# Layer 2's mixing: four stores and then four loads, or one store and one load by turns, on the transfer queue of a four-layer convolution kernel

## The chip, the cores and the metric

The kernel runs on one core of a Trainium2 chip. The metric is the device time of one execution, in microseconds. Before the change it is 4314.44 us, the median of 3 runs (4307.86 to 4318.33).

The core has five engines with a queue of instructions each: TensorE (PE in the profile, with its weight loads as PEld), VectorE (DVE), ScalarE (ACT), GpSimd (POOL) and SyncE (SP). They run side by side and wait for each other with semaphores. SP does no arithmetic here; it issues transfers, which 16 DMA engines then carry out. A transfer that has to wait holds up everything that stands behind it on SP.

## The reference

A tensor x of 16 samples, 16 channels and 256 x 256 points, in float32, goes through four layers. Each normalises x in groups (8 groups over 16 channels), convolves it in its own way and adds the result to x:

```
x = x + _L0_conv_ref(_gn(x), L0_conv_weight)          # 3x3, circular, by FFT in the reference
x = x + _L1_conv_ref(_gn(x), L1_conv_filter_w)        # five diagonal taps
x = x + _L2_conv_ref(_gn(x), ty, tx, poles, residues) # spectral layer with poles
x = x + _L3_conv_ref(_gn(x), weight, scale, bias)     # 3x3 on rounded inputs
```

The change lies in layer 2:

```
alpha = jnp.fft.fft2(x, axes=(-2, -1))
A = 1.0 / (omega1[:, None, None, None] - weights_pole1[None])
Bm = 1.0 / (omega2[:, None, None, None] - weights_pole2[None])
S = jnp.einsum('ikpq,oikp,xikq->oxik', weights_residue, A, Bm)
output_residue1 = jnp.einsum('biox,oxik->bkox', alpha, S)
...
x1 = jnp.fft.ifft2(output_residue1, s=(Ny, Nx), axes=(-2, -1)).real
```

At each frequency (o, x) the 16 input channels of every sample are mixed by a 16 x 16 complex matrix S(o, x), which is itself made of poles and residues. This mixing, output_residue1, is the stage that the change touches. A second term (x2, from C, D and output_residue2) is made elsewhere.

## The kernel before

The function layers holds the whole kernel as stages one after another: layers 0 and 1 together, sample by sample; layer 2's forward transform; layer 2's mixing; layer 2's way back; and layer 3.

The forward transform leaves alpha in a DRAM tensor alphad, by row frequency. There are 256 of these, as real and imaginary parts of the even and odd halves of the spectrum. The mixing takes them in NF = 64 blocks of 4. It writes the mixed spectrum to a DRAM tensor mixd, which the way back reads (tile ot, line 1148), so the way back begins only when the mixing's stores are done.

**One block of the mixing** (the loop over n from line 963). The block's data lie in a tile z, of which there are two, zs[0] and zs[1], used by turns. z has 128 partitions. The four frequencies of a block lie in every fourth partition, each in its own quarter of the columns, and the rest is zero, so that one product mixes four frequencies at once. Line 970 is this product:

```
nc.tensor.matmul(to, lhsT=sk[:, x_], rhs=z[:, :, x_], start=True, stop=True)
```

It runs for each of 129 column frequencies x_: 128 in the loop over at (32 steps of four), and one alone. Every product of a block reads all partitions of z, so a block's first product needs all four of its loads. After each 8 steps (g = 0 to 3) ACT copies half of the sums from PSUM (other, line 996) and DVE adds and subtracts (line 998, which the profile shows under the helper's line 190) into the output tile ob, of which there are two as well. POOL corrects a few elements of ob (lines 1007 to 1010).

**The mixing matrices** are made in the same loop, two blocks ahead, by the generator system: products of line 891, copied from PSUM into sk by ACT and DVE by turns (lines 899 to 908), with POOL copying one part (line 905). Another generator, poles, makes factors of the matrices on POOL and DVE. The loop advances both with next(...) between its own steps.

**The transfers of a block**, all on SP:

- load (lines 915 to 918) brings one of the four frequencies: alphad into z, 32 partitions by 2064 numbers, 258 KB. reload (lines 927 to 931) is the load with a marker ahead of it: DVE sets one element of z to zero (line 930), so the load waits until DVE has come to this place and the older products that read this z are done. During block n, reload fetches the data of block n + 1, into the z that block n does not use.
- leave (lines 920 to 925) stores a quarter of ob: 64 partitions by 1024 numbers, 256 KB, into mixd.

In the program's text they stand like this. For block n (from n = 1), after step group g = 0: reload(n + 1, 0), leave(n - 1, 1), reload(n + 1, 1), leave(n - 1, 2). After g = 1: reload(n + 1, 2), leave(n - 1, 3), reload(n + 1, 3). After g = 3: leave(n, 0). Below, S0 to S3 are the four stores of block n - 1 and L0 to L3 the four loads for block n + 1.

**What sets the order.** A scheduler may reorder each engine's instructions within what the data allow. A context, tc.manual_schedule, lists engines for which the order of the program's text is kept. In the mixing (line 935) the list names PE, DVE, ACT and POOL. SP isn't in it, so the scheduler sets SP's order. It puts the four stores of a block together and then the four loads:

```
L924 mixd<-ob x4     S0 S1 S2 S3 of block n-1
L917 z<-alphad x4    L0 L1 L2 L3 for block n+1, each waits for its marker on DVE
L924 mixd<-ob x4     the next block
```

Of the kernel before, what the change touches and what calls it, by code (L numbers as in the profile page):

```python
# [164 lines left out]
def layers(ctx, tc, x, w0, w1, w3, sw, bias, ty, tx, p1a, p1b, p1c, p2a, p2b, p2c, resa, resb,  # L165
# [695 lines left out]
    with ExitStack() as es:  # L861
# [65 lines left out]
        def reload(n, f):  # L927
# [5 lines left out]


        es.enter_context(tc.manual_schedule(engines={
            mybir.EngineType.PE, mybir.EngineType.DVE, mybir.EngineType.Activation, mybir.EngineType.Pool}))

        zs = [new(zp, [FB, NX, BG], f"z{k}") for k in range(2)]
        V.memset(zs[0][:, 0 : FB // 2], 0.0)
# [485 lines left out]
```

## Time and profile before

| what | value |
|---|---|
| median of 3 runs | 4314.44 us |
| the profiled execution's own time | 4332.44 us |
| its span | 4330.7 us |
| busy over the span: PE, DVE, ACT, POOL | 86%, 70%, 59%, 47% |
| mixing: first and last start of a product of line 970 | 2272.5 and 3013.4 us |
| transfers in the mixing: loads of z, stores of ob | 258, 256 |
| median time from issue to landing: loads, stores | 4.0 us, 4.5 us |
| the marker of line 930 on DVE | 59 ns |
| issue of a load, of a store on SP (median) | 478 ns, 590 ns |

How to read it: the profile is one execution. Its page gives each engine's busy time, groups of equal instructions by line, and for each group the idle time before it with the instruction or transfer that ended it ("releaser"). "issue" as a releaser means that nothing in the profile explains the wait. A transfer appears twice: as an instruction on SP's queue (the issue) and, by its semaphore, as the landing that others wait for. The views used further on are the page, the busy times in a stretch of time ("windows"), the waits by who waited for whom, the instructions in order of time, and the list of transfers. The first block (n = 0) reloads and stores nothing of this kind and the last (n = 63) loads nothing, so that 62 blocks (n = 1 to 62) have the full set of four stores and four loads.

### The profile page before, as it was taken

How to read it: one execution, taken by the hardware profiler on the slowest of the kernel's cores; microseconds unless marked ns; L12 is line 12 of the kernel's file. 1: busy time of each engine (PE TensorE's matmuls, PEld its weight loads, DVE VectorE, ACT ScalarE, POOL GpSimd, SP SyncE). 2: the span in 40 equal slices, each digit the busy share in tenths (PEclk: the TensorE clock that was granted, in tenths of full speed). 3: DMA queues.
4: the chain of work that ended last, by engine and by line, in shares of the span. 5: the costliest groups of instructions: out<-in, count | busy, mean ns of one | idle time of the engine just before them, and what ended most of it. 6: DMA issues, size and time to landing. Idle time of an engine off the chain costs nothing. (4 is left out here: it accounts for less than half of the span.)

```text
span 4330.7 us, 126404 instructions
## 1 busy us (share of the span) xinstructions
PE 3739.1 (86%) x52880; PEld 2882.1 (67%) x52880; DVE 3040.5 (70%) x5585; ACT 2573.2 (59%) x3641; POOL 2057.0 (47%) x3279
## 2 busy tenths in 40 slices
PE   4999999999967989999996777776899999996776
PEld 1455555555545989899985555555788888883444
DVE  4676667666659878787765566664567777768888
ACT  2868686776824434344446666665545544447898
POOL 2233232423244645564546666664566666662222
PEclk9999999999988999999999999998999999997989
DMA  6767676776633544444535666666878888877998
GB/s 141 172 154 191 142 192 150 183 169 155 158 89 117 164 144 144 139 152 157 162 113 167 182 194 183 185 192 174 228 217 239 237 244 235 247 206 273 343 351 295
DMA packets 479579, 820.78 MB, mean 190 GB/s; under 512 B 39648, under 2 KB 371424, under 8 KB 463584
## 3 DMA queue, kind: packets, MB, share of 16 engines
q1 hardware_dynamic: 431904, 644.63, 52.6%
q0 software_dynamic: 47104, 168.06, 13.0%
q8 instruction: 416, 6.82, 0.7%
q14 instruction: 155, 1.27, 0.1%
HBM read 408.85 MB, written 336.07 MB: 172 GB/s over the span
## 5 line engine op out<-in xcount | busy, mean ns | idle before, releaser
L382 PE MATMUL ps<-va,wt 128*64 128x512 f32 (+1 forms) x1632 | 668.7, 571 | 11.6 <-POOL va L354 9.2
L382 PE MATMUL ps<-vb,wt 128*64 128x512 f32 (+1 forms) x1632 | 667.1, 570 | 4.5 <-DMA vb<-va 4.5
L781 ACT ACTIVATE y<-ps_y,bc 128x384 f32<-128x384 f32 x512 | 296.4, 581 | 406.8 <-PE ps_y L779 406.6
L403 ACT ACTIVATE v<-xt,nm 32x2048 f32<-32x2048 f32 x248 | 497.2, 2005 | 9.8 <-PE ps L417 3.5
L417 PE MATMUL ps<-v,w1s 128*64 128x259 f32 x4096 | 486.4, 397 | 11.0 <-DVE v L401 6.7
L970 PE MATMUL ps_m<-z,sk 128*32 128x64 f32 x16384 | 334.5, 227 | 176.1 <-issue 126.5
L190 POOL TENSOR_TENSOR w<-rq 128x512 f32<-128x512 f32 x256 | 335.7, 1333 | 261.5 <-ACT rq L1115 259.4
L970 PEld LDWEIGHTS ps_m<-z,sk 128*32 128x32 f32 x16384 | 302.9, 114 | 227.2 <-issue 151.9
L382 PEld LDWEIGHTS ps<-va,wt 128*64 128x64 f32 x1632 | 223.1, 137 | 311.3 <-issue 283.3
L417 PEld LDWEIGHTS ps<-v,w1s 128*64 128x64 f32 x4096 | 338.9, 142 | 136.0 <-issue 27.9
L1114 PE MATMUL ps_o<-exp,fs 128*128 128x128 f32 x2048 | 399.6, 277 | 9.7 <-ACT fs L1162 9.7
L1113 PE MATMUL ps_o<-c_last,zt 128*128 128x128 f32 x2048 | 398.1, 276 | 0.0
L190 DVE TENSOR_TENSOR ob<-ps_m,other 128x256 f32<-128x256 f32 x512 | 192.9, 418 | 276.0 <-ACT other L996 262.4
L1259 PE MATMUL ps_c<-q,wt 64*64 64x512 bf16 (+1 forms) x4608 | 292.8, 405 | 108.6 <-ACT o L1306 91.7
L1113 PEld LDWEIGHTS ps_o<-c_last,zt 128*128 128x128 f32 x2048 | 323.2, 193 | 60.8 <-issue 60.8
L891 PE MATMUL ps_s<-t,l 128*32 128x258 f32 x4096 | 320.5, 401 | 42.3 <-issue 24.8
L190 POOL TENSOR_TENSOR acc<-acc,prod 128x256 f32<-128x256 f32 x240 | 232.8, 970 | 226.4 <-DVE prod L190 220.3
L1259 PEld LDWEIGHTS <-wt 64*64 64x64 bf16 x4800 | 181.6, 114 | 220.2 <-issue 152.8
L1114 PEld LDWEIGHTS ps_o<-exp,fs 128*128 128x128 f32 x2048 | 313.7, 194 | 11.3 <-ACT fs L1162 11.3
L776 PE MATMUL ps_y<-c_y,qd 128*128 128x128 f32 x2048 | 316.0, 277 | 1.6 <-ACT hat L738 1.6
L779 PE MATMUL ps_y<-hat,qd 128*128 128x128 f32 x2048 | 314.5, 276 | 0.0
L190 DVE TENSOR_TENSOR xt<-xt,ps 128x512 f32<-128x512 f32 x256 | 175.4, 685 | 187.6 <-PE ps L382 185.6
(234 smaller groups left out, 8897.9 us busy)
## 6 DMA issues: line engine op xcount, KB each, us to landing
xt<-x2d SPq DMA_DIRECT2D x256, 512.0 KB, 4.3
z<-alphad SPq DMA_DIRECT2D x258, 258.0 KB, 4.0
xt<-in_x_dram SPq DMA_DIRECT2D x256, 256.0 KB, 7.4
x2d<-x2s POOLq DMA_DIRECT2D x256, 256.0 KB, 5.0
mixd<-ob SPq DMA_DIRECT2D x256, 256.0 KB, 4.5
ot<-mixd SPq DMA_DIRECT2D x256, 256.0 KB, 6.2
x3d<-xt SPq DMA_DIRECT2D x128, 512.0 KB, 5.4
xt<-x3d SPq DMA_DIRECT2D x64, 1024.0 KB, 9.4
```

What stands on the lines that cost most here:

```text
L190: eng.tensor_tensor(o, a, b, op)
L382: nc.tensor.matmul(ps[halves[h], lo:hi, :], lhsT=wt0[:, w, :], rhs=v[:, 2 * t + lo : 2 * t + hi, j : j + N], start=j == 0 and k == 0, stop ...
L403: nc.scalar.activation(to, o.xt[c][q_], AF.Identity, bias=o.g.nm[q_, 1:2])
L417: nc.tensor.matmul(ps[halves[h], k, 0:U], lhsT=o.w1[:, w : w + 64], rhs=v1[:, lo : lo + U], start=first_, stop=not first_)
L776: nc.tensor.matmul(to[:, :, a, :], lhsT=v[:, c, a, i % 2, :], start=a == 0, stop=a == 1, rhs=y1[:, a].rearrange("p (r f) -> p r f", r=2))
L779: nc.tensor.matmul(ps[:, 2 * P : 3 * P], lhsT=v[:, c, a, i % 2, :], start=False, stop=a == 1, rhs=hats[0][:, a, i].rearrange("p r k -> p ( ...
L781: nc.scalar.activation(y[:, c, :], ps[:, 0 : 3 * P], AF.Copy, scale=bc2[:, b, i // 2, 0:1])
L891: nc.tensor.matmul(ps[at : at + 32, d, 0 : 2 * NX], lhsT=ls[h][:, k + d - k0, n], rhs=t2[:, h, k + d].rearrange("p r x -> p (r x)"), start ...
L970: nc.tensor.matmul(to, lhsT=sk[:, x_], rhs=z[:, :, x_], start=True, stop=True)
L1113: nc.tensor.matmul(ps[:, a, c, :], lhsT=zts[d][:, a, c, :], rhs=last[:, c, :], start=True, stop=False)
L1114: nc.tensor.matmul(ps[:, a, c, :], lhsT=fs[:, d, a, :], rhs=ey[:, d, c, :], start=False, stop=True)
L1259: nc.tensor.matmul(o, lhsT=wt[half[h], w, :], rhs=src, start=i == 0, stop=i == len(work[0]) - 1)
```

## The change

SP is added to the engines whose order is the program's own, in the mixing stage only. SP's order becomes S0 L0 S1 L1 S2 L2 S3 L3 for the blocks that have all eight, 62 of them; before these and after them the queue stands as before. The other engines keep the order of their instructions, and the rest of the kernel is not touched. Since one line is added, the lines behind it are one higher in the changed kernel's profile (L970 becomes L971; L917, L924 and L930 lie ahead of the added line and keep their numbers).

```
@@ -933,7 +933,8 @@
         es.enter_context(tc.manual_schedule(engines={
-            mybir.EngineType.PE, mybir.EngineType.DVE, mybir.EngineType.Activation, mybir.EngineType.Pool}))
+            mybir.EngineType.PE, mybir.EngineType.DVE, mybir.EngineType.Activation, mybir.EngineType.Pool,
+            mybir.EngineType.SP}))
```

The queue of the changed kernel, for a block:

```
L924 mixd<-ob     S0 of block n-1
L917 z<-alphad    L0 for block n+1, waits for its marker on DVE
L924 mixd<-ob     S1
L917 z<-alphad    L1, waits for its marker
L924 mixd<-ob     S2
L917 z<-alphad    L2, waits for its marker
L924 mixd<-ob     S3
L917 z<-alphad    L3, waits for its marker
```

## The prediction

> **What bounds the kernel now.** I read the page's head first, then its groups (which line belongs to which stage), then the stretch of the mixing alone, then in that stretch PE's waits and the transfer queue's order of time, and last single transfers.
>
> ```profile
> span 4330.7 us, 126404 instructions
> PE 3739.1 (86%) x52880; PEld 2882.1 (67%) x52880; DVE 3040.5 (70%) x5585; ACT 2573.2 (59%) x3641; POOL 2057.0 (47%) x3279
> ```
>
> The whole kernel is PE's, but the change touches one stage, from the first product of L970 (2272.5 us) to the last (3013.4 us). The windows view of that stretch has the busy times, in the order PE, PEld, DVE, ACT, POOL, then granted clock, DMA share, GB/s:
>
> ```profile
> 2272.00:3014.00 742.00, 531.80 (x20470) 429.56 (x20464) 435.91 (x1261) 496.06 (x1188) 451.71 (x1061) 0.96 0.63 183
> ```
>
> No engine is full: PE 72%, ACT 67%, DMA 63%. 64 blocks in 742 us are 11.6 us each, so a cycle of waits sets the pace. PE's waits from 2290 us to the stretch's end (total, times, longest):
>
> ```profile
> PE ps_m L970 <- issue: 126.5, 89, 3.9
> PE ps_m L970 <- ACT sk L908: 31.2, 30, 1.7
> PE ps_s L891 <- issue: 24.8, 19, 2.1
> PE ps_m L970 <- DMA z<-alphad: 15.0, 16, 2.2
> ```
>
> The largest is "issue", 151.3 us in 108 waits; the wait for z seems small. The queue's order of time and single transfers say more. One block, first the queue, then its fourth load alone, then that load's time to landing, then the first load's, then PE:
>
> ```profile
> 2601.99 3.12 SPq L924 DMA_DIRECT2D mixd<-ob  x4
> 2605.21 6.32 SPq L917 DMA_DIRECT2D z<-alphad  x4
> 2614.75 2.75 SPq L924 DMA_DIRECT2D mixd<-ob  x4
> ...
> 2611.09 0.45 SPq L917 DMA_DIRECT2D z<-alphad  x1
> ...
> z<-alphad SPq DMA_DIRECT2D x1, 258.0 KB, 2.9
> ...
> z<-alphad SPq DMA_DIRECT2D x1, 258.0 KB, 4.8
> ...
> 2614.11 0.89 PE L970 MATMUL ps_m<-z,sk 128*32 128x64 f32 x49
> ```
>
> The fourth load is issued at 2611.09, lands 2.9 us later at 2613.97, and 0.14 us after that the next block's first product starts. The loop is: a block's products, DVE's second pair of sums and the fourth marker (L930, at 2611.00), fourth load, next block. PE's wait table hides it, because other matmuls stand between and the gap is then written to another releaser. Taking the landing of every fourth load from the trace's semaphore events, 26 of 62 blocks start 0.13 to 0.14 us after it (28 within 0.25 us); the other 34 have 0.36 to 2.8 us of slack. So in nearly half of the blocks the last load's landing is the pace. It is issued 7.2 us after the block's start, at DVE's pace, and lands 3.5 us later in the mean; alone it would take 2.9, the rest is queueing.
>
> **The change part by part.** No compute instruction is added, removed or moved; PE, DVE, ACT and POOL keep their order. What moves is 3 of 4 stores in each of 62 blocks, on SP's queue alone (POOL issues no transfer in this stage, and the last block's four stores, which the next stage reads, stay where they are): S0 S1 S2 S3 L0 L1 L2 L3 becomes S0 L0 S1 L1 S2 L2 S3 L3.
>
> *Gain for the loads.* L0 no longer stands behind three stores' issue. Before, its marker comes 2.3 us after the block's start and its issue some 0.15 to 0.4 us later. But L0 isn't what the next block waits for; L3 is. Worth nothing, and no other cover is needed for it.
>
> *Issue time on SP.* L1, L2 and L3 each get one store issue (median 590 ns) ahead of them. L2 and L3 wait for markers 2.9 and 1.9 us after the one before, so these issues fit in. L1 comes some 0.5 us later and has 3 us to spare. Worth nothing for L3.
>
> *Stores are held by the loads' markers.* S1, S2, S3 wait behind L0, L1, L2 for DVE's L930. S0 goes at -0.3 us from the block's start as before; S1 moves from 0.3 to about 3.1, S2 from 0.9 to about 4.3, S3 from 1.6 to about 5.9. Before, four stores used the stretch from 0 to 5 us, in which no load can run yet; now only one does, and three quarters of a megabyte is put among the loads, ahead of L3. That is the cost. It needs the service time of a transfer in a full queue. From the block above: the fourth store lands 4.9 us after its issue (2603.78), 6.7 us after the first one's issue; less 3.05 for a lone transfer that is three services of 1.2 us. My estimate from the landings of all 62 blocks (mean miss 0.37 us) is a queue served in order, 3.05 us for a lone transfer, 1.2 us a store, 0.85 us a load. Then, from a block's start: L0 issued at 2.6, lands at 5.65; S1 6.85, L1 7.7, S2 8.9, L2 9.75, S3 10.95, L3 11.8. Before, L3 lands at 7.3 + 3.5 = 10.8. It comes 1.0 us later.
>
> Bounds of that delay. From below: the transfer packets' own time fills 63% of the engines, 7.2 us a block, 0.9 us for each of eight transfers. Six services of 0.9 after L0 give 11.05, and with an L0 at 2.4 about 10.9: +0.1 to +0.5. Nothing below zero: L3's issue is bound by the same marker, and the same bytes stand ahead of it, later. From above: replayed block by block with the fitted services, against the same replay of the old order, the mean delay is 1.55 us.
>
> Price: a block is pushed by the delay less its slack. With 1.0 us: 28 blocks by nearly 1.0 (27.8 us) and 19 blocks with slacks of 0.36 to 1.11 by the rest (8.7 us), 36 us. With 0.5 us: 15 us. With 1.5 us: 61 us.
>
> *What is won back.* [...] 151.3 of 742 us is a fifth, so I take a fifth off: 36 becomes 28 us. The ends are nothing (36) and a loop in which every block runs at the queue's floor of 11.8 + 0.14 us, against 11.55 now: 62 x 0.4 = 25 us, or 13 us with an L3 at 11.6.
>
> *Stores' release of ob.* ob has two buffers; block n+1's first sums wait for the four stores of block n-1. Before, these have 6.8 us to spare in the median, 5.0 at least. S3's landing moves by about 4.7 us (6.4 to 11.0), so 0.3 to 2 us are left. Taken as nothing; in the upper end it isn't.
>
> [...]
>
> [...]
>
> **Sum.** +28 us on the profiled execution, whose own time is 4332.4 us (span 4330.7), 18 us above the median of the runs, 4314.4. On the median: 4342 us, 0.65% slower. About 0.3%, 13 us, is what a measurement of this kernel can tell from no change.
>
> **The rivals.**
>
> 1. *The queue drains in time, nothing changes.* For it: DMA is only 63% busy, and late in the block packets are sparse. Then L3 takes its 2.9 to 3.5 us as before: 4314 us, give or take 8. Against: L0, behind four stores, takes 4.8 us where L3 takes 2.9; a load pays for stores ahead of it.
>
> 2. *Faster.* In the first 3 us of a block the transfer engines have one store in place of four, and PE's instruction fetch, which uses them too (the page's third part has a queue of kind instruction), is quicker there. Place: "issue" gaps that begin 1 to 4 us into a block, about 39 of the 151 us by the trace. If half of that went and L3 kept its landing, 20 us: 4295 us. It decides once L3's delay is under about 0.3 us. Against: fetches come at every phase of a block, and the freed transfers return at 4 to 11 us, where about 100 us of the gaps lie.
>
> 3. *Slower by more: S3 comes too late for ob.* DVE's L190 sums into ob then wait for the stores, which no row shows today, and the markers behind them on DVE, hence all loads, move with them. It decides where S3 lands over 5 us later than now. At 0.5 us in each of 62 blocks it adds 31 us to the upper 61: about 4400 us.
>
> **How the numbers follow.** Forecast (L3 late by 0.5 to 1.5 us): 0.68, 4328 to 4375, middle 4342. Rival 1: 0.16. Rival 2: 0.09. Rival 3: 0.07. The range 4312 to 4383 leaves out rival 2, the lower part of rival 1 and most of rival 3, about 2 in 10. Slower by over 0.3%: nearly all of the forecast and rival 3, 0.73. Within: rival 1 and the forecast's lowest part, 0.18. Faster: 0.09.
>
> **What the profile after would show.** Right: the queue's order of time has stores and loads by turns; the wait of PE's L970 for DMA z<-alphad grows from 15.0 us to 30 or more; the loads' median time to landing falls for the first and rises for the fourth to over 4 us; well over 28 blocks start 0.14 us after their fourth load; the stage grows from 742 to about 770 us while busy times stay, and every other stage keeps its time. "Issue" falls a little. Wrong: the fourth load still lands in 3.5 us or less (rival 1), or "issue" falls by 20 us and more (rival 2), or DVE's ob waits for DMA mixd<-ob (rival 3).

## The result: 1.5% slower, all of it in the mixing

The changed kernel takes 4375.73 us (median of 4 runs, 4372.4 to 4387.79) against 4311.15 us before (median of 4, 4307.47 to 4318.33). The ratio is 1.0153, with a 95% interval of 1.0128 to 1.0177. The forecast was 4342 us: right in sign and inside its range, but 28 us of loss where there are 65.

The profiled execution took 4387.79 us, with a span of 4386.0 us. Its page begins:

```profile
span 4386.0 us, 126404 instructions
PE 3778.1 (86%) x52880; PEld 2905.2 (66%) x52880; DVE 3036.9 (69%) x5585; ACT 2569.5 (59%) x3641; POOL 2052.7 (47%) x3279
```

The busy times of DVE, ACT and POOL are those of before. The windows view, over the mixing and over all that follows it (busy PE, PEld, DVE, ACT, POOL; granted clock, DMA share, GB/s), places the loss. The last line is the kernel before, over what follows its mixing:

```profile
2268.00:3071.00 803.00, 570.65 (x20467) 452.87 (x20464) 434.51 (x1260) 493.51 (x1186) 448.75 (x1060) 0.91 0.57 169
3071.00:4386.00 1315.00, 1146.23 (x17348) 923.96 (x17348) 980.15 (x1343) 799.11 (x1034) 675.68 (x518) 0.94 0.83 259
...
3014.00:4330.70 1316.70, 1141.57 (x17348) 920.91 (x17348) 980.54 (x1343) 799.90 (x1034) 674.33 (x516) 0.94 0.85 258
```

The mixing has grown from 741.0 to 802.7 us, from its first product's start to its last one's end. What follows takes 1315.0 us, where it took 1316.7, and the mixing begins at 2268.0 us, where it began at 2272.5. PE's busy time in the stage rose by 39 us and its granted clock fell from 0.96 to 0.91; more on that below.

PE's waits from 2290 us on, that is from the stage's second block (total, times, longest):

```profile
PE ps_m L971 <- issue: 90.8, 74, 3.0
PE ps_m L971 <- DMA z<-alphad: 78.8, 40, 4.1
PE ps_s L891 <- issue: 18.8, 16, 3.1
```

The wait for z has gone from 15.0 to 78.8 us; "issue" has gone from 151.3 to 109.6. One block in order of time, first SP's queue, then the fourth load's time to landing, then PE's first product of the next block:

```profile
2613.39 0.45 SPq L917 DMA_DIRECT2D z<-alphad  x1
2613.89 0.59 SPq L924 DMA_DIRECT2D mixd<-ob  x1
2614.57 0.55 SPq L917 DMA_DIRECT2D z<-alphad  x1
2615.17 0.71 SPq L924 DMA_DIRECT2D mixd<-ob  x1
2615.96 0.56 SPq L917 DMA_DIRECT2D z<-alphad  x1
2616.57 0.90 SPq L924 DMA_DIRECT2D mixd<-ob  x1
2617.57 1.45 SPq L917 DMA_DIRECT2D z<-alphad  x1
...
z<-alphad SPq DMA_DIRECT2D x1, 258.0 KB, 4.8
...
2622.58 1.10 PE L971 MATMUL ps_m<-z,sk 128*32 128x64 f32 x64 [1.97 <-DMA z<-alphad]
```

By turns, as announced. L3 is issued at 2617.57, lands 4.8 us later (2622.34 by its semaphore), and the next block starts 0.24 us after that. PE has been idle for 1.97 us by then. By the semaphore events, 52 of 62 blocks now start within 0.3 us of their last load's landing; before it was 28.

Mean times in the 62 blocks, in us from a block's first product (issue on SP, then landing), from the events of the two traces:

| | S0 | S1 | S2 | S3 | L0 | L1 | L2 | L3 | next block |
|---|---|---|---|---|---|---|---|---|---|
| before, issue | -0.23 | 0.29 | 1.07 | 1.79 | 3.00 | 3.91 | 5.55 | 7.33 | 11.55 |
| before, landing | 2.93 | 4.19 | 5.37 | 6.55 | 7.38 | 8.10 | 9.30 | 10.82 | |
| after, issue | -1.39 | 3.37 | 4.74 | 6.52 | 2.87 | 4.12 | 5.91 | 7.68 | 12.56 |
| after, landing | 1.70 | 7.07 | 9.78 | 11.40 | 5.87 | 8.91 | 10.72 | 12.19 | |

L3 lands 1.37 us later. 0.35 us of that is a later issue (behind S3's), the rest is time in the queue: 4.51 us from issue to landing against 3.49. The block is 1.01 us longer; 62 x 1.01 is 62.6 us, and the stage as a whole grew by 61.7.

### The profile page after: what moved, and what is told of

The parts are those of the page before. It is cut to its first block, busy times and chain, and to the rows that moved or that the text cites. A ratio compares the mean times of both kernels' runs of the same rounds, so it can differ in the third digit from the quotient of the medians.

```text
span 4386.0 us, 126404 instructions
## 1 busy us (share of the span) xinstructions
PE 3778.1 (86%) x52880; PEld 2905.2 (66%) x52880; DVE 3036.9 (69%) x5585; ACT 2569.5 (59%) x3641; POOL 2052.7 (47%) x3279
## 5 line engine op out<-in xcount | busy, mean ns | idle before, releaser
L971 PE MATMUL ps_m<-z,sk 128*32 128x64 f32 x16384 | 349.2, 235 | 197.0 <-issue 90.8
L971 PEld LDWEIGHTS ps_m<-z,sk 128*32 128x32 f32 x16384 | 317.4, 119 | 250.8 <-issue 151.8
L1115 PE MATMUL ps_o<-exp,fs 128*128 128x128 f32 x2048 | 400.8, 278 | 10.8 <-ACT fs L1163 10.8
L891 PE MATMUL ps_s<-t,l 128*32 128x258 f32 x4096 | 339.1, 417 | 43.9 <-POOL l L190 22.7
```

The lines of the kernel that those rows point to most:

```text
L891: nc.tensor.matmul(ps[at : at + 32, d, 0 : 2 * NX], lhsT=ls[h][:, k + d - k0, n], rhs=t2[:, h, k + d].rearrange("p r x -> p (r x)"), start ...
L1115: nc.tensor.matmul(ps[:, a, c, :], lhsT=fs[:, d, a, :], rhs=ey[:, d, c, :], start=False, stop=True)
```

## Experiments

Three theories. **A**: a block starts when its last load has landed, and in the new order seven transfers have to be moved between L0's marker and that landing. **B**: stores that are held back cost as such, by the late release of ob, or by mixing stores and loads in the transfer engines. **C**: L3 is late because of its own late marker and the one store just ahead of it. The edit of every kernel is shown against the changed kernel, unless said otherwise, with the ratio to the kernel before on the same chip. In these runs the kernel before has a median of 4323 to 4325 us, so 0.1% is 4.3 us. Times within a block are means over the 62 blocks of the run's trace, as in the table above.

### The last store behind the last load

S0 L0 S1 L1 S2 L2 L3 S3:

```
-                        leave(n - 1, 2 * g + 1)
+                    if n and g == 0:
+                        leave(n - 1, 1)
...
                         reload(n + 1, 2 * g + 1)
-                    if n and g == 0:
-                        leave(n - 1, 2)
+                        leave(n - 1, g + 2)
```

> One store moved out of the last load's way: S0 L0 S1 L1 S2 L2 L3 S3. Theory A (a full queue served in order, the last load's landing sets the block's start): in the changed kernel L3 is issued 7.7 us into a block and lands at 12.2; without S3 ahead of it, it is issued at its marker (7.3) and lands one store's service earlier, at about 11.0, still a little later than the 10.8 of the kernel before. Time 4320 to 4338 us, three quarters of the loss gone. Theory B (the loss is in the stores: late release of ob, or a queue that stands at markers): S3 is later still, time stays at 4370 us or rises.

Ratio 1.0107 (1.0081 to 1.0134). L3 lands at 11.70 and the mean block is 12.20 us. PE's wait for z in this run:

```profile
PE ps_m L971 <- DMA z<-alphad: 31.3, 20, 2.7
```

Neither expectation was met in size: a third of the loss is gone, not three quarters and not nothing. L3 gained 0.49 us, where a whole service of 1.2 us was expected: S3 had cost L3 only about half a microsecond, and four transfers still stand between L0 and L3.

### All markers after the first group of sums

The changed kernel's order, but L1 to L3 no longer wait for the second group:

```
-                    if n and g < 2:
-                        reload(n + 1, 2 * g)
-                        leave(n - 1, 2 * g + 1)
+                    if n and g == 0:
+                        reload(n + 1, 0)
+                        leave(n - 1, 1)
...
-                    if n and g < 2:
-                        reload(n + 1, 2 * g + 1)
                     if n and g == 0:
-                        leave(n - 1, 2)
+                        for f in range(1, 4):
+                            reload(n + 1, f)
+                            if f < 3:
+                                leave(n - 1, f + 1)
```

> Order of the changed kernel, S0 L0 S1 L1 S2 L2 S3 L3, but all four markers on DVE after the first group of sums (2.7 us into a block), so that no load waits for the second group. Theory A (service in order: six transfers stand between L0 and L3's landing, so the last landing is bound by bytes and not by its marker): L3 still lands 11.7 to 12.2 us into a block, time 4360 to 4380 us. Theory C (L3 is late because its marker at 7.3 us comes late and S3 is issued just ahead of it): L3 is issued at about 6.5, lands before 11, time back at 4300 to 4325 us.

Ratio 1.0149 (1.0124 to 1.0173): the changed kernel's loss, unchanged. The fourth marker came at 2.84 us instead of 7.29, and L3 still was issued at 7.37 and landed at 12.24. SP itself took from 2.95 to 7.37 us to come from L0's issue to L3's: L0's issue took 0.45 us, those of the six behind it 0.56 to 0.92 us in the mean. This is theory A's outcome (a little beyond its 4380 us and 12.2 us) and excludes C's marker: the last landing is bound by the transfers ahead of it.

### The same markers with four stores and then four loads

```
-                    if n and g < 2:
-                        reload(n + 1, 2 * g)
-                        leave(n - 1, 2 * g + 1)
+                    if n and g == 0:
+                        reload(n + 1, 0)
...
-                    if n and g < 2:
-                        reload(n + 1, 2 * g + 1)
                     if n and g == 0:
-                        leave(n - 1, 2)
+                        for f in range(1, 4):
+                            reload(n + 1, f)
                     if g == 3:
-                        leave(n, 0)
+                        for part in range(4):
+                            leave(n, part)
...
```

> Four stores and then four loads as in the kernel before, but all four markers after the first group of sums. Theory A: the queue runs from the first store on without a gap, S3 lands at 6.4 us into a block, L3 at 6.4 + 4 x 0.85 = 9.8, one us earlier than before. The 26 blocks that started 0.14 us after L3 are no longer paced by it; time 4285 to 4303 us. Theory C expects the same gain or more, since L3's marker is 4.5 us earlier. If the time is that of the kernel before (4311 within 8), the landing of L3 was not the pace there and theory A is in doubt.

Ratio 1.0015 (1.0002 to 1.0029). L3 lands at 10.27, not at 9.8, but 0.55 us earlier than in the kernel before, and the wait for z is nearly gone, yet nothing is gained:

```profile
PE ps_m L971 <- issue: 153.7, 99, 3.4
PE ps_m L971 <- ACT sk L908: 25.4, 25, 1.7
PE ps_s L891 <- issue: 25.2, 18, 2.2
PE ps_m L971 <- DMA z<-alphad: 5.3, 5, 2.6
```

"issue" took the place: 178.9 us, from 151.3. This contradicts a step of the prediction: the 26 blocks that started right after L3's landing were not held back by it in sum. It is also the outcome for which the expectation itself put theory A in doubt, and for the kernel before A does not hold: there is a second floor, 11.55 to 11.6 us a block, made of PE's work and its "issue" time, and z's landing lay at about the same level. Where L3 lands later, as in the changed kernel, A is not touched by this.

### The turns, begun at the block's start

The changed kernel's order with all markers ahead of the first group of sums:

```
+            if n:
+                for f in range(4):
+                    reload(n + 1, f)
+                    if f < 3:
+                        leave(n - 1, f + 1)
             for at in range(PX):
...
-                    if n and g < 2:
-                        reload(n + 1, 2 * g)
-                        leave(n - 1, 2 * g + 1)
...
-                    if n and g < 2:
-                        reload(n + 1, 2 * g + 1)
-                    if n and g == 0:
-                        leave(n - 1, 2)
```

> Order S0 L0 S1 L1 S2 L2 S3 L3, with all four markers at the block's start, ahead of the first group of sums on DVE. Theory A: the same queue as in the changed kernel begins 2.7 us earlier, L3 lands at 9.0 to 9.7 us into a block and no longer sets its end; time 4285 to 4320 us, although every store still stands among the loads. Theory B (stores among loads cost as such, by contention or by late stores): time stays above 4340 us.

Ratio 1.0000 (0.9985 to 1.0015). The order is the changed kernel's, every store but S0 stands among the loads, and the loss is gone: L0 is issued at 0.64 instead of 2.87 and L3 lands at 10.20. That is later than the 9.0 to 9.7 expected, and the 4323 us lie just over A's 4320, but far from B's 4340. PE's waits:

```profile
PE ps_m L971 <- issue: 140.2, 93, 3.5
PE ps_s L891 <- issue: 26.6, 17, 3.3
PE ps_m L971 <- ACT sk L908: 19.6, 20, 1.7
PE ps_m L971 <- DMA z<-alphad: 8.8, 8, 2.4
```

Mixing stores and loads costs nothing by itself (against B): from S0's issue to L3's landing the eight transfers take 10.18 us here and 10.23 us as four stores and four loads in the experiment above. What costs is that the queue starts at a marker 2.7 us into the block and then needs 9.3 us.

### The last load late, with no store near it

Four stores and then four loads; L3's marker one group of sums later. The stores are moved as in the experiment with four stores and four loads; the edit of the markers:

```
-                    if n and g < 2:
-                        reload(n + 1, 2 * g + 1)
+                    if n and g in (0, 2):
+                        reload(n + 1, 1 + g)
```

> Four stores and then four loads as in the kernel before, no store among the loads, but the fourth load's marker one group of sums later (after g = 2 and the work behind it, about 9.3 us into a block instead of 7.2). Theory A (the block's start follows the landing of the last load, whatever made it late): L3, alone in the queue, lands at about 12.3, as in the changed kernel; mean block 12.5 to 12.8 us, time 50 to 75 us above the kernel before, z waits of 60 us or more, and the granted clock in the stage falls as it did in the changed kernel. Theory B (the loss comes from stores and loads being mixed in the transfer engines, or from a lower clock of its own): a loss under 25 us, and no fall of the clock.

Ratio 1.0050 (1.0033 to 1.0068), about 22 us. The marker came at 8.38 us, not at 9.3, so L3 landed at 11.61 and not at 12.3; the block is 11.94 us. By its numbers (a loss under 25 us, no fall of the clock) this is theory B's outcome, but the load was late by only half of what was planned. With L3 0.79 us later than in the kernel before, the block is 0.39 us longer, and 49 of 62 blocks start within 0.3 us of L3's landing, where 28 did. So a late landing alone, without any store near it, makes a loss:

```profile
PE ps_m L971 <- DMA z<-alphad: 36.0, 26, 2.3
```

The clock hardly fell (0.957 over the 62 blocks, 0.963 before). That part of theory A's expectation failed.

### One store held back

S0 S1 S2 L0 L1 L2 S3 L3, the change for one store alone:

```
-                        leave(n - 1, 2 * g + 1)
...
                     if n and g < 2:
+                        if g:
+                            leave(n - 1, 3)
                         reload(n + 1, 2 * g + 1)
-                    if n and g == 0:
-                        leave(n - 1, 2)
                     if g == 3:
-                        leave(n, 0)
+                        for part in range(3):
+                            leave(n, part)
```

> Part of the change alone: S0 S1 S2 L0 L1 L2 S3 L3, one store held back to just ahead of the last load, the other three as in the kernel before. Theory A (the last load's landing, made late by all that the queue still has to move after L0): the queue has time for one store between L2's and L3's markers, L3 lands at 10.7 to 11.1 us into a block against 10.8 before and 12.2 in the changed kernel; loss 0 to 12 us. Theory C (what costs is the store directly ahead of L3, its issue and its service): half of the changed kernel's loss or more, 30 us and up.

Ratio 1.0042 (1.0023 to 1.0061), 18 us. L3 landed at 11.50, 0.4 later than the most I expected, and the block is 11.90 us. 18 us is less than theory C's 30 and more than A's 12. The store just ahead of the last load does cost something by itself, although it is issued 1.3 us ahead of L3: it lands at 10.27, and L3 1.23 us after it.

### Three stores behind the loads

S0 L0 L1 L2 L3 S1 S2 S3:

```
-                        leave(n - 1, 2 * g + 1)
...
-                    if n and g == 0:
-                        leave(n - 1, 2)
+                    if n and g == 1:
+                        for part in range(1, 4):
+                            leave(n - 1, part)
```

> S0 L0 L1 L2 L3 S1 S2 S3: three stores later than in any kernel so far, but none ahead of a load. Theory A: L3 is issued at its marker and lands at about 10.3 us into a block; S3 lands at about 12.8, still ahead of the next sums into its ob at 13.5; time within 10 us of the kernel before. The floor there is not z (moving the markers alone gained nothing), so no gain either. Theory B (stores made late cost as such): the loss of the changed kernel or more, 60 us and up.

Ratio 1.0044 (1.0027 to 1.0060), 19 us. Both theories missed. L3 landed at 11.39, not 10.3, S3 at 14.54, not 12.8, and DVE's sums now wait for S3 (DVE's waits in this run):

```profile
DVE ob L190 <- ACT other L997: 167.1, 119, 6.5
DVE ob L190 <- DMA mixd<-ob: 119.3, 46, 5.9
```

In 51 of 62 blocks the sums into ob start 0.22 us after the last store has landed, and the fourth marker, behind them on DVE, comes at 7.96 us instead of 7.22. This is the prediction's third rival, late stores that hold up ob, and here it is real. In the changed kernel it isn't: there the sums come at least 2.4 us after the last store, and DVE's waits for mixd<-ob are 0.4 us in all.

### One load of four

What is the floor under z? Against the kernel before:

```
-                load(n, f, f)
+                if n < 2 or f == 0:
+                    load(n, f, f)
```

> The order of the kernel before, with three of the four loads of each block left out from the third block on (z keeps older numbers there, so the mixing is done on stale data), all markers kept. It takes the z wait away and 0.77 MB of 2.06 MB of transfers a block. Theory F (PE's unexplained 'issue' time is its instruction stream, held up by the data transfers): 'issue' falls from 150 us to under 100 and the mean block from 11.55 to about 11.0 us, 30 us or more faster than before. Theory P ('issue' is PE's own pace and does not depend on transfers): 'issue' stays at 150 to 180 us as it did when only the markers were moved, and the time stays within 10 us of the kernel before.

Ratio 0.9876 (0.9854 to 0.9897), 54 us faster; the mean block is 10.68 us. PE's waits:

```profile
PE ps_m L971 <- issue: 104.4, 87, 2.9
PE ps_m L971 <- ACT sk L908: 26.1, 27, 1.7
PE ps_s L891 <- issue: 17.5, 22, 1.4
```

"issue" falls to 121.9 us, where with z out of the way and all transfers in place it was 178.9. The 100 us of theory F were not reached, but 57 us of "issue" go away, and the time goes with them; theory P is out. One thing besides the loads differs: S2 and S3 now stand behind L0 on the queue, because SP's order is again the scheduler's.

What stands ahead of the end of an "issue" gap, the traces show. The profile has a queue of kind instruction (packets, MB, share). In the kernel before, from 2290 to 3014 us, and then one "issue" gap of PE:

```profile
q8 instruction: 158, 2.59, 1.4%
...
2607.29 0.58 PE L970 MATMUL ps_m<-z,sk 128*32 128x64 f32 x26 [2.04 <-issue]
```

A packet of this queue, 16 KB, ran from 2605.07 to 2606.00 us, and the gap ended 1.29 us after it. All 107 "issue" gaps of PE in the 62 blocks, 150.5 us, end 1.13 to 1.61 us after such a packet has landed; a moment taken at random lies so in 11% of cases. So do, within 1.15 to 1.70 us, all 115 of the kernel with all markers at g = 0 and four stores ahead of four loads, and all 108 of this run. The profile does not say for which engine a packet is. No gap stands without one; that PE waits for its instructions there is the author's reading of these times, and no run shows it by itself. The floor is taken as PE's work and its "issue" gaps. Without the three loads the gaps are as many and shorter, 1.09 us in the mean instead of 1.41 (1.54 with all markers at g = 0). By which path the data transfers lengthen them is not shown: a packet itself takes 0.96 us before and 0.97 here (medians).

### All kernels together

In order of L3's landing (means over the 62 blocks), without the two kernels that have another bound (three stores behind, one load of four):

| order | L3 lands | block | ratio |
|---|---|---|---|
| turns, markers at the start | 10.20 | 11.57 | 1.0000 |
| four and four, markers at g = 0 | 10.27 | 11.60 | 1.0015 |
| before | 10.82 | 11.55 | 1 |
| one store held | 11.50 | 11.90 | 1.0042 |
| four and four, L3's marker late | 11.61 | 11.94 | 1.0050 |
| last store behind | 11.70 | 12.20 | 1.0107 |
| changed | 12.19 | 12.56 | 1.0153 |
| turns, markers at g = 0 | 12.24 | 12.65 | 1.0149 |

Two floors: 11.55 to 11.6 us from PE's work and its "issue" time, and, in the five rows at the bottom, L3's landing plus 0.33 to 0.50. The block has the higher one. No kernel that computes the whole result beat the kernel before: with z out of the way, in the two rows at the top, the block is no shorter than before.

## Why the prediction was right in sign and mechanism, and wrong in size

**The mechanism held.** Stores held by the loads' markers crowd into the stretch ahead of L3, L3 lands late, and z's landing becomes the pace of nearly every block. Most signs that the prediction named for this are there: the z wait grew (78.8 us for "30 or more"), well over 28 blocks start right after L3 (0.24 us after it, not 0.14), the first load lands sooner and the fourth takes more than 4 us, and the other stages kept their time. Two are not: PE's busy time rose by 39 us where busy times were to stay, and "issue" fell by 42 us, which the prediction had named as rival 2's sign. Rival 2's gain did not come with it.

**The steps that failed** are two terms of the sum: the delay of L3, put at 1.0 us, and the fifth that was taken off as won back. The stage grew by 61.7 us, 34 more than the 28 of the sum. Of these, 8 are the fifth, about 23 the delay (by the prediction's own rule for the price, 1.0 us costs 36 and the measured shift 59), and the rest is open.

**The bound before** was read wrongly in one point. 26 blocks that start 0.14 us after a landing look as if that landing were their price. Taking it away gained nothing, since PE's "issue" filled the same time. The two floors lay close together, and the events show only which came last.

**The delay of L3** was the mis-sized term: 1.0 us forecast, 1.37 measured, inside the bounds of 0.1 to 1.55. L0's issue was put at 2.6 us and came at 2.87: its marker, put at 2.3 us, comes at 2.39 in the block shown, but at 2.69 in the mean of the kernel before. From L0's landing to L3's it was 6.15 us forecast, 6.32 measured. The single steps were less good than their sum: L1 lands 1.84 us after S1 instead of 0.85, S3 0.68 after L2 instead of 1.2. The fitted services were right as an average of about 1.05 us a transfer in a full queue, not for a store and a load apart, and the first experiment, priced with a store's 1.2 us, missed for this reason. The replay block by block, which the prediction used only as the upper bound (1.55), was nearer than the hand sum. The "+0.5" of the lower bound does not follow from its figures: 11.05 less 10.8 is 0.25.

**The price.** A push of 1.37 us plus a start that is 0.1 us slower gives 28 x 1.47 and the rest of the slacks, 59 us, by the prediction's own rule. The stage lost 61.7. The agreement is not luck: for the four other kernels of the table that land L3 late, the rule gives 23, 27, 36 and 63 us (estimates from the slacks of the kernel before), and their stages grew by 23.2, 26.1, 40.0 and 67.4. It holds in one direction only. With L3 0.55 us earlier, blocks that the landing paced should have gained, and the stage did not get shorter (745.8 us).

**What is won back** failed outright: a fifth was taken off, which no run shows, and nothing came back. "issue" did fall, by 42 us, but PE's wait for z rose by 64 (15.0 to 78.8 us) and the stage grew by 61.7. Once z paces the block, less "issue" only leaves PE waiting longer for z. It would have had a worth only with "issue" as the pace.

**The rivals.** The queue did not drain in time. Rival 2's sign came true without its gain: 90 "issue" gaps of 1.22 us in the mean, where there were 107 of 1.41. That instructions came faster is not shown: a packet of theirs takes 0.96 us in both kernels (medians). Late ob did not occur here and does occur when the stores move further back.

**Transfers and "issue", as measured.** In the changed kernel L0, in an empty queue, took 3.0 us, and the six transfers behind it took 1.05 each. The 107 "issue" gaps of the kernel before, each behind a packet of the instruction queue, are 150.5 us of the 716 us of 62 blocks.

## What to carry to other kernels

A transfer that waits for a marker also holds everything behind it on its queue (S1, behind L0, was issued at 3.37 us into a block instead of 0.29): before stores and loads are mixed, ask which transfer the next block waits for, and how many bytes now stand between its release and its landing. Order alone cost nothing here when the queue began earlier, and a late last load alone cost 22 us without any mixing. When two floors lie close together, a wait that seems to pace half of the blocks may be worth nothing to remove and most of its length to extend: L3 0.55 us earlier gained nothing here, and 1.37 us later it cost 1.01 us a block.

## What the runs showed of the hardware

**Stretches at half speed stand behind gaps of PE.** In the 62 blocks the granted clock is 0.963 before and 0.912 after; the clock records have half speed in stretches of 3.41 us or twice that, 53 us in all before and 137 us after. Of the 16 stretches before, 15 follow a gap of PE of 2.0 to 2.6 us and one a gap of 3.9; all 32 after follow a gap of at least 1.8. The reverse does not hold: seven other gaps before, of 2.0 to 2.5 us, have no such stretch behind them. The 84 us more at half speed lengthen PE's work by an estimated 42 us, half of them, which is about its 39 us of extra busy time. It is an effect of the loss far more than its cause. From L0's issue to L3's landing the queue needs 9.3 of the 12.56 us of a block, and what PE's pace can move in it, the markers, hardly moved: L0's comes at 2.73 us after and 2.69 before, the fourth at 7.29 and 7.22. The turns begun at the block's start ran their 62 blocks at a clock of 0.948, with 75 us at half speed, and lost nothing; with L3's marker late the loss came at 0.957. What the clock adds in the ten blocks that L3's landing does not pace was not tried.

**The order of waits shows.** PE takes the waits of a block's first product one after another: in the block of the changed kernel shown above, the records of the last two start 0.213 and 0.107 us ahead of the product. Where the wait for L3 is the last wait instruction (the kernel before, one store held, L3's marker late), a paced block starts 0.135 us after the landing. In the kernels with stores and loads by turns one more stands behind it, for L0, which landed 6 us earlier, and it is 0.241; with three stores behind the loads two more do, and it is 0.352. At 52 blocks the 0.106 us are some 5 us of the loss. It was not tested apart.

**PE's "issue" gaps end behind packets of the instruction queue.** Each of the 107 in the kernel before ends 1.13 to 1.61 us after a 16 KB packet of the instruction queue, as told with the experiment on one load of four.
